# Causal attention and a routed mixture of experts: another order of query halves in the first and the last element, and a lead of the maxima that rises and falls

## The chip, the cores and the metric

The kernel runs on one core of a Trainium2 chip. The metric is the device time of one execution in microseconds (us). A kernel's time is the median of several executions; a profile comes from one execution.

## The reference

The input is x, 4 elements of 1,024 tokens with 256 channels. Attention has 16 heads of 16 channels; its weights are low-rank pairs (down to 64, up to 16), and half of each head's channels of q and k are rotated by position. Then each token goes to two of eight experts. In short:

```
q, k, v = heads of x through down and up, rotary on half of q's and k's channels
scores  = q k^T / sqrt(16), masked to k <= q
y       = softmax(scores) v, joined over the heads
x       = layernorm(x + y Wc)

scores  = (x router_w^T + router_b) / max(temperature, 0.1)       # 8 experts
gates   = exp(sinkhorn(scores, 3 rounds over tokens' and experts' axes, per element))
top two gates of each token, normed to a sum of 1
out     = sum over the two: gate * (relu(x wg_e) * (x wp_e)) wo_e   # 256 -> 512 -> 256
x       = layernorm(x + out)
```

The Sinkhorn rounds and the gates of an element need all of its 1,024 tokens. The experts need all gates of an element.

## The kernel before

**Projection.** Element b is projected in two halves of 512 tokens (project(b, half)). x comes transposed from memory, is split into a high and a low part for matmuls in three terms, and q and k are made and cut into three bf16 pieces each, since later matmuls over the pieces give fp32 precision. The pieces (lv) are written to a scratch in device memory, parts[b], by six DMAs for each half: on SP's queue for element 0, on POOL's for the others. The elementwise steps named lean run on DVE for element 0 and on POOL for the others. v stays on the chip, in va[b % 2].

**Stacks.** Attention is done in units. A unit is an element, one or two groups of four heads, and one or both halves of the queries. load_stack(unit) (L336) reads its pieces back from parts into the tiles qs[i] and ks[i], with i the unit's number modulo 3: 12 DMAs on SP for a one-group unit, 24 for a two-group unit. So the loads of unit i + 3 wait until unit i's matmuls have read the same tiles. load_stack for unit i + 2 is called early in unit i, and at step 30 where unit i + 2 is the first of the next element.

**Maxima.** For each group and half, row_max computes all the scores once, with queries on the partitions (s, L354), and DVE takes the row maxima (L360 off the diagonal, L363 on it). They are transposed, split and written as two more rows of qs by DMAs on ACT's queue. The maxima run ahead of the attention by LEAD steps. A step is one head of one block of 128 keys against 512 queries in the attention, or one head with 128 queries in the maxima.

**Attention.** attend(unit) makes the scores again, with keys on the partitions and minus the maximum included (sT, L433). ACT takes exp into a tile pT (L437), which has three buffers, each with four heads of one key block kb. Diagonal blocks are masked by an affine_select on POOL (L446), or in the last NDV = 2 units by a minimum on DVE (L442). Then come the matmuls y (L417), two blocks behind, and ACT copies the finished y to yT (L422). Keys of block kb with the second half's queries are diagonal for kb 4 to 7.

The units before are: elements 0 to 2, a unit for each group with both halves, 48 steps each; element 3, two units of two groups with the first half of queries (32 steps each), then four units of one group with the second half (32 steps each). In all there are 768 steps.

**Work beside attention.** Two lists of generators are advanced step by step, by budgets. The lane holds the projection of later elements (P), prepare (constants, and the clearing of the pair lists), and finish of the element before (F: transposing y, the output projection, layernorm and the router's scores). The side holds route (R: Sinkhorn, the top two, and the places of the pairs) and lay_out (T: which expert each slot of 256 rows belongs to). The last step of route is 16 scatters of pairs to device memory (L808), on POOL's queue. They are issued only while `hole` is true, in the first eight steps of a second-half part, and in_turn keeps them behind the diagonals that were already emitted on POOL:

```
at = n - HG * BPQ * (len(qcs) - 1)
hole[0] = qcs[-1] > 0 and HOLE[0] <= at < HOLE[1]
```

A scheduler orders the instructions of each engine; every engine then works through its own in order. The maxima have a higher priority.

**The end.** After attention, finish of the last half runs alone, then the last element's route and lay_out, and the slots: 39 slots of 256 rows, of which 35 are always run. Each loads its expert's weights (w), its pairs (ent) and rows (xg), and does gp and eo matmuls. The first 17 slots hold rows of elements 0 to 2 only, and begin right after attention (first gp matmul at 703.7 us in the profile).

Of the kernel before, what the change touches and what calls it, by code (L numbers as in the profile page):

```python
# [17 lines left out]
R_BUFS, X1_BUFS, PT_BUFS, SIDE, SCAT = (1,2,3,0.035,0.07)  # L18
W_BUFS, GA, EA, EO = (2,3,4,6)
SIDE3 = 0.2  # L20
BUD3 = ((8,0,8,0),(4,4,8,8))
YB = 2
XG = 3
SCAT3 = 0.4
# [4 lines left out]
NDV = 2  # L29
HOLE = (0,8)  # L30
PR = (200,0,0)
LEAD = 44
PSUM = bass.MemoryType.PSUM
DRAM = bass.MemoryType.DRAM

P = 128
# [7 lines left out]
def kernel(  # L44
# [189 lines left out]
    def project(b, half, tile_):  # L234
        if half == 0:
            parts[b] = dram.tile([2, NQC, 3, DH, H, QC], BF16, name=f"parts{b}", tag="parts", bufs=2)
        pd = parts[b]
        n = f"{b}_{half}"
        xh = x_half.pop((b, half))
        cols = slice(half * QC, (half + 1) * QC)  # L240
        lean = nc.gpsimd if b else nc.vector
        hi = proj.tile([P, CC, QC], F32R, tag="xT_h", name=f"xT_h{n}")
        lo = proj.tile([P, CC, QC], F32R, tag="xT_l", name=f"xT_l{n}")
        for c in range(CC):
            split(hi[:, c], lo[:, c], xh[:, c], lean)
        yield 0.2
        if half + 1 < NQC or b + 1 < B:
            load_x(b + (half + 1) // NQC, (half + 1) % NQC)

        def chunk(k):  # L250
            ps = tile_(f"qk_ps{n}_{k}")
            cut = slice(k * P, (k + 1) * P)
            mm3(ps, [(wqk_h[:, c, cut], wqk_l[:, c, cut], hi[:, c], lo[:, c]) for c in range(CC)])
            return ps

        def store(k, src, sub, rows):

            lv = proj.tile([P, 3, QC], BF16, tag=f"lv{k}", name=f"lv{n}_{k}")
            nc.scalar.copy(lv[:, 0], src)
            r = proj.tile([P, QC], F32, tag="r", name=f"r{n}_{k}", bufs=R_BUFS)  # L260
            sub.tensor_tensor(r, src, lv[:, 0], ALU.subtract)
            nc.scalar.copy(lv[:, 1], r)
            lean.tensor_tensor(lv[:, 2], r, lv[:, 1], ALU.subtract)
            at = 0
            for qk, row, m in rows:
                (nc.gpsimd if b else nc.sync).dma_start(
                    out=pd[qk, half, :, row : row + m].rearrange("k d h t -> (d h) k t"),
                    in_=lv[at : at + m * H],
                )
                at += m * H  # L270

        for qk in range(2):
            store(2 + qk, chunk(2 + qk), nc.vector, [(qk, 0, DHE)])
            yield 1.3
        pair = []
        for o in range(2):
            pair.append(chunk(o))
            yield 1.3
        for o in range(2):
            t1 = proj.tile([P, QC], F32, tag="t1", name=f"t1_{n}_{o}", bufs=R_BUFS)  # L280
            nc.vector.tensor_tensor(t1, pair[o], rope[:, 2 * o, cols], ALU.mult)
            t2 = proj.tile([P, QC], F32, tag="t2", name=f"t2_{n}_{o}", bufs=R_BUFS)
            nc.vector.tensor_tensor(t2, pair[1 - o], rope[:, 2 * o + 1, cols], ALU.mult)
            lean.tensor_tensor(t1, t1, t2, ALU.add)
            store(o, t1, lean, [(qk, DHE + o * DHE // 2, DHE // 2) for qk in range(2)])
            yield 0.2
        while b >= 2 and not attended.get(b - 2):
            yield WAIT
        dst = va[b % 2][:, half * BPQ : (half + 1) * BPQ, : H * VW]
        for i in range(0, BPQ, 2):  # L290
            ps = tile_(f"v_ps{n}_{i}")
            for j in range(2):
                tok = slice((i + j) * P, (i + j + 1) * P)
                mm3(
                    ps[:, j * C : (j + 1) * C],
                    [(hi[:, c, tok], lo[:, c, tok], wv_h[:, c], wv_l[:, c]) for c in range(CC)],
                )
            for j in range(2):
                nc.scalar.copy(
                    dst[:, i + j].rearrange("p (h d) -> p h d", d=VW)[:, :, :DH],  # L300
                    ps[:, j * C : (j + 1) * C].rearrange("p (h d) -> p h d", d=DH),
                )
            yield 1.3

    units = [(b, (g,), tuple(range(NQC))) for b in range(B - 1) for g in range(NG)]
    units += [(B - 1, (g, g + 1), (0,)) for g in range(0, NG, 2)]
    units += [(B - 1, (g,), (qc,)) for qc in range(1, NQC) for g in range(NG)]

    def stack(unit, g):

# [85 lines left out]
    def attend(unit):  # L398

        b, gs, qcs = unit  # L400
        for g in gs:
            if qcs == (0,):
                y = late_pool[0].tile([P, QC], F32, name=f"yT{b}_{g}_0")
            else:
                y = work.tile([P, T], F32, tag=f"yT{g}", name=f"yT{b}_{g}", bufs=2 if g == 0 else 1)
            for qc in qcs:
                yT[b, g, qc] = y[:, qc * QC : (qc + 1) * QC]
        acc = {}
        behind = []

# [652 lines left out]
                    break  # L1063

    drain(project(0, 0, any_tile))
    load_stack(units[0], (0,))
    drain(project(0, 1, any_tile))
    load_stack(units[0], (1,))
    load_stack(units[1])
    maxima = (1 if step is None else step for u in units for step in row_max(u))  # L1070
    early = project(1, 0, bg_tile)
    attended_to = maxed = 0
    for n in range(HG * BPQ + 1):
        maxed += next(maxima)
# [1 line left out]
            next(early, None)  # L1076

    lane, side = Lane(), Lane()
    lane.add("P1", early)
    lane.add("P1", project(1, 1, bg_tile))  # L1080
    lane.add("prepare", prepare())
    budget = {0: (8.0, 8.0, 8.0, 11.3), 1: (9.5, 9.5, 6.0, 11.3), 2: (9.5, 9.5, 6.0, 0.0)}
    order = [(0, s) for s in range(NA)] + [(1, s) for s in range(NSLOT - NA)]
    sure, more = order[:SURE], order[SURE:]
    early = None

    routed = [0]
    for i, unit in enumerate(units):
        b, gs, qcs = unit
        g = gs[0]  # L1090
        last = b == B - 1
        if g == 0 and qcs[0] == 0 and b > 0:
            if b == 1:
                lane.until("P2h0")
            elif b == 2:
                lane.until("P3h0")
            lane.add(f"F{b - 1}", finish(b - 1))
            if b + 1 < B:
                lane.add(f"P{b + 1}", project(b + 1, 1, bg_tile))
            if last:  # L1100
                lane.until(f"P{b}")
                pctx.close()
                late_pool[0] = pctx.enter_context(tc.tile_pool(name="late", bufs=1, reuse_waits="tile"))
        if g == 1 and 0 < b < B - 1 or g == 0 and last and qcs[0] == 1:
            lane.until(f"F{b - 1}")
        if g == 0 and last and qcs[0] == 1:
            lane.add("F", finish(b, (0,)))
        if g == 3 and b + 2 < B:
            lane.add(f"P{b + 2}h0", project(b + 2, 0, bg_tile))
        steps = len(gs) * sum(HG * BPQ * (qc + 1) for qc in qcs)  # L1110
        give = BUD3[qcs[0]][g] if last else budget[b][g]
        for n, over in enumerate(attend(unit)):
            attended_to += not over
            if i + 2 < len(units):
                if units[i + 2][0] != units[i + 1][0]:
                    if n == 30:
                        lane.until(f"P{b + 1}")
                        load_stack(units[i + 2])
                elif n == 4:
                    load_stack(units[i + 2])  # L1120

            while maxed < min(attended_to + LEAD, HG * BPQ + 3 * attended_to):
                with tc.high_priority(offset=PR[0]):
                    step = next(maxima, None)
                if step is None:
                    break
                maxed += step
            with tc.high_priority(offset=PR[1]):
                lane.give(give / steps)
            if routed[0] < b and not any(m == f"F{b - 1}" for m, _ in lane.todo):  # L1130
                routed[0] = b
                side.add("R", route(b - 1))
                if last:
                    side.add("T", lay_out(0))
            at = n - HG * BPQ * (len(qcs) - 1)
            hole[0] = qcs[-1] > 0 and HOLE[0] <= at < HOLE[1]
            with tc.high_priority(offset=PR[2]):
                side.give(SIDE3 if last else SIDE)
            if last and routed[0] == b and not side.todo and early is None:
                early = pctx.enter_context(early_pool())  # L1140
                fetch(sure[:NA], 0)
        if gs[-1] == NG - 1:
            attended[b] = True
    hole[0] = True
    side.until("T")
    lane.until("F")
# [5 lines left out]
    actx.close()  # L1152
    experts = ctx.enter_context(ExitStack())
    ffn = experts.enter_context(ffn_pool())
    for gen in (finish(B - 1, (1,), alone=True), route(B - 1), lay_out(1)):
        drain(gen)
    filled = nc.values_load(
        tables["filled"][0:1, 0:1], min_val=0, max_val=NSLOT - NA,
# [156 lines left out]
```

## Time and profile before

| what | us |
|---|---|
| time, median of 3 (1090.1 to 1093.66) | 1090.66 |
| the profiled execution's own time | 1088.8 |
| its span | 1087.1 |
| PE busy | 974.8 |
| DVE busy | 821.6 |
| ACT busy | 707.8 |
| POOL busy | 492.4 |
| first load of a stack on SP | 37.1 |
| first s, first sT | 46.5, 66.1 |
| the last yT copy (end of attention) | 702.6 |

Span is the time between the first and the last instruction of the profile, and the mean granted clock of TensorE in it is 0.968 of full speed. Busy times of different engines overlap. An engine's idle time costs nothing unless what it waits for is on the chain that sets the end. Times of single instructions are those of this execution, counted from the start of the span. PEld is TensorE's loading of the fixed operand, which overlaps its matmuls.

### The profile page before, as it was taken

The page shows a single profiled execution, that of the slowest core. Times are in us where ns is not written, and L with a number is a line of the kernel's source. Part 1 is how long each engine was busy: PE and PEld are TensorE (multiplying, and loading weights), DVE is VectorE, ACT ScalarE, POOL GpSimd, SP SyncE. Part 2 cuts the span into 40 slices and gives each one's busy share as a digit, 9 for nine tenths or more (in the row PEclk, how much of TensorE's full clock was granted, in tenths as well). Part 3 has the DMA queues.
Part 4 walks back from the last instruction along what each step waited for, and adds up shares of the span by engine and source line. Part 5 has one row for each costly group of instructions (what it writes and reads, how often), then busy time and mean ns, then how long its engine had stood idle before and what let it go on. Part 6 is the DMA issues. An engine that isn't in the chain of part 4 may idle for free.

```text
span 1087.1 us, 20881 instructions
## 1 busy us (share of the span) xinstructions
PE 974.8 (90%) x6808; PEld 616.2 (57%) x6808; DVE 821.6 (76%) x2551; ACT 707.8 (65%) x1701; POOL 492.4 (45%) x552
## 2 busy tenths in 40 slices
PE   6689999999989999999899999999999699999940
PEld 4444333355434345533344333499999699999940
DVE  4768778888897888887538997398897588888716
ACT  3446666666776665676566776777776577877723
POOL 7167511121443624440423414645557756666545
PEclk9889999999999999999999999999999899999975
DMA  7663411231331312421123220587873788899638
GB/s 258 178 210 112 118 49 35 79 96 44 106 90 48 109 46 74 142 54 50 50 84 121 47 64 2 179 252 214 227 222 101 230 235 237 230 237 255 148 42 309
DMA packets 92065, 146.33 MB, mean 135 GB/s; under 512 B 19760, under 2 KB 55088, under 8 KB 91568
## 3 DMA queue, kind: packets, MB, share of 16 engines
q1 hardware_dynamic: 69296, 108.50, 31.6%
q0 software_dynamic: 20608, 36.18, 14.3%
q8 instruction: 56, 0.92, 0.3%
q10 hardware_dynamic: 2048, 0.27, 0.2%
q14 instruction: 57, 0.47, 0.1%
HBM read 109.26 MB, written 35.38 MB: 133 GB/s over the span
## 4 chain that ended last, share of the span: by engine, by line
PE 68%; DVE 8%; DMA 7%; ACT 6%; issue 4%; POOL 4%; SPq 2%; ACTq 0%; DVEq 0%; POOLq 0%
PE y L417 13%; PE s L354 10%; PE sT L433 9%; PE gp L195 5%; PE gp L196 5%; PE gp L197 5%; ACT pT L437 4%; POOL pairs L808 3%; PE eo L195 3%; PE eo L196 3%; PE eo L197 3%; PE po L591 2%; DVE mx L360 2%; DMA results<-eo,ent 2%; SPq L336 2%
## 5 line engine op out<-in xcount | busy, mean ns | idle before, releaser
L437 ACT ACTIVATE pT<-sT 128x512 f32<-128x512 f32 (+3 forms) x768 | 346.9, 491 | 178.4 <-PE sT L433 151.0
L363 DVE CUSTOM_DVE_ANT_0 d<-s,mask 128x128 bf16<-128x128 f32 (+3 forms) x512 | 237.0, 482 | 51.4 <-PE s L354 50.2
L433 PE MATMUL sT<-qs,ks 98*128 98x512 bf16 (+3 forms) x768 | 231.7, 328 | 16.4 <-ACT pT L437 11.6
L354 PE MATMUL s<-ks,qs 96*128 96x512 bf16 (+3 forms) x768 | 221.9, 331 | 22.5 <-DVE mx L363 7.8
L446 POOL TENSOR_SCALAR_AFFINE_SELECT pT<-pT 128x512 f32<-128x512 f32 x120 | 76.4, 637 | 273.1 <-ACT pT L437 256.8
L360 DVE TENSOR_REDUCE mx<-s 128x1 f32<-128x512 f32 x256 | 175.1, 684 | 29.4 <-PE s L354 28.3
L417 PE MATMUL y<-pT,va 128*32 128x512 f32 (+3 forms) x1536 | 181.9, 500 | 2.0 <-POOL pT L446 0.9
L1010 POOL DMA_INDIRECT results<-eo,ent x70 | 116.9, 1670 | 107.3 <-ACT hh L188 22.1
L189 DVE TENSOR_TENSOR wl<-w,wh 128x512 fp32r<-128x512 f32 x210 | 134.9, 685 | 37.7 <-ACT wh L188 37.4
L195 PE MATMUL gp<-xh,wh 128*128 128x256 f32 x560 | 159.5, 286 | 1.3 <-ACT xh L188 0.7
L197 PE MATMUL gp<-xh,wl 128*128 128x256 f32 x560 | 158.6, 284 | 0.5 <-DVE wl L189 0.5
L196 PE MATMUL gp<-xl,wh 128*128 128x256 f32 x560 | 158.9, 284 | 0.0
L354 PEld LDWEIGHTS <-qs 96*128 96x128 bf16 x768 | 71.6, 99 | 132.8 <-issue 101.0
L433 PEld LDWEIGHTS <-ks 98*128 98x128 bf16 x768 | 71.8, 98 | 122.9 <-issue 91.2
L188 ACT CAST wh<-w 128x512 fp32r<-128x512 f32 x210 | 117.6, 621 | 12.7 <-DMA w<-in_wg_dram 10.9
L195 PEld LDWEIGHTS gp<-xh,wh 128*128 128x128 f32 x560 | 106.0, 190 | 2.4 <-ACT xh L188 1.2
L197 PEld LDWEIGHTS gp<-xh,wl 128*128 128x128 f32 x560 | 106.3, 190 | 0.8 <-DVE wl L189 0.7
L196 PEld LDWEIGHTS gp<-xl,wh 128*128 128x128 f32 x560 | 106.3, 190 | 0.0
L929 POOL DMA_INDIRECT xg<-x_rows,ent x70 | 79.6, 1137 | 37.1 <-issue 17.4
L195 PE MATMUL eo<-wh,hh 128*128 128x256 f32 x280 | 80.1, 286 | 10.4 <-ACT hh L188 9.0
L808 POOL DMA_INDIRECT pairs<-ent,so_i x64 | 66.5, 1039 | 29.6 <-issue 18.4
L196 PE MATMUL eo<-wl,hh 128*128 128x256 f32 x280 | 79.1, 283 | 0.0
(207 smaller groups left out, 1603.1 us busy)
## 6 DMA issues: line engine op xcount, KB each, us to landing
w<-in_wg_dram SPq DMA_DIRECT2D x35, 512.0 KB, 6.2
w<-in_wp_dram SPq DMA_DIRECT2D x35, 512.0 KB, 5.6
w<-in_wo_dram SPq DMA_DIRECT2D x35, 512.0 KB, 4.7
ks<-parts SPq DMA_DIRECT2D x90, 128.0 KB, 2.8
qs<-parts SPq DMA_DIRECT2D x66, 128.0 KB, 2.9
parts<-lv POOLq DMA_DIRECT2D x12, 384.0 KB, 3.1
parts<-lv POOLq DMA_DIRECT2D x24, 192.0 KB, 3.1
xh<-in_x_t_dram SPq DMA_DIRECT2D x8, 512.0 KB, 5.8
```

The lines of the kernel that those rows point to most:

```text
L188: nc.scalar.copy(hi, src)
L189: (sub or nc.vector).tensor_tensor(lo, src, hi.bitcast(F32), ALU.subtract)
L195: nc.tensor.matmul(ps, lhsT=sh, rhs=mh, start=(i == 0), stop=False)
L196: nc.tensor.matmul(ps, lhsT=sh, rhs=ml, start=False, stop=False)
L197: nc.tensor.matmul(ps, lhsT=sl, rhs=mh, start=False, stop=(i == n - 1))
L354: nc.tensor.matmul(ps[:, :w], lhsT=q(h, half)[:NROW, t * P : (t + 1) * P], rhs=k(h, k0 // QC)[:NROW, :w], start=True, stop=True,)
L360: nc.vector.tensor_reduce(m, ps, AX.X, ALU.max)
L363: nc.vector.tensor_tensor_reduce(out=dump[:, :w], in0=ps[:, :w], in1=mask[:, QC - w :], scale=1.0, scalar=MASKED, op0=ALU.add, op1=ALU.max ...
L417: nc.tensor.matmul(acc[g, qc][SLOT * h : SLOT * (h + 1), lo:], lhsT=va[b % 2][:, kb, at : at + SLOT], rhs=pT[:, h, lo:], start=(kb == 0), ...
L433: nc.tensor.matmul(st[:, lo:], lhsT=k(h, kb // BPQ)[: NROW + 2, kb % BPQ * P : (kb % BPQ + 1) * P], rhs=q(h, qc)[: NROW + 2, lo:], start=T ...
L437: nc.scalar.activation(pT[:, h, lo:], st[:, lo:], AF.Exp, scale=scale)
L1010: ins = nc.gpsimd.indirect_dma_start(out=results[:, :], out_offset=bass.IndirectOffsetOnAxis(ap=ent[:, j, 1:2], axis=0), in_=eo, in_offset ...
```

## The change

Element 0 now has the units that element 3 had: two units of two groups with the first half of queries (firsts), then four of one group with the second half (others). Its attention is begun after only the first half has been projected. The second half's projection becomes the first item of the lane, with its lean steps on POOL, and has to be done at step 26 of unit 0, where the loads of unit 2 are issued. The loads of units 0 and 1 (24 DMAs each) are issued before that.

Element 3 has the same units in the other order: the four with the second half of queries first, the two with the first half last. With that, the half that finish takes inside attention is the second and the half that it takes alone is the first. The last two units, which cut their diagonals on DVE, are now the two firsts.

The lead of the maxima is 22 steps at the start, rises by 0.35 for each step of attention to 44, and falls again near the end, from 44 to 22, where it stays for the last 64 steps. Before, it was 44, with a cap of 16 and three for each step at the start. The budgets of the lane are listed by the number of the unit in its element.

```diff
-BUD3 = ((8,0,8,0),(4,4,8,8))
...
-LEAD = 44
+LEAD, SLIM = 44, 22
...
-        lean = nc.gpsimd if b else nc.vector
+        lean = nc.gpsimd if b or half else nc.vector
...
-    units = [(b, (g,), tuple(range(NQC))) for b in range(B - 1) for g in range(NG)]
-    units += [(B - 1, (g, g + 1), (0,)) for g in range(0, NG, 2)]
-    units += [(B - 1, (g,), (qc,)) for qc in range(1, NQC) for g in range(NG)]
+    firsts = [((g, g + 1), (0,)) for g in range(0, NG, 2)]
+    others = [((g,), (qc,)) for qc in range(1, NQC) for g in range(NG)]
+    units = [(0, *u) for u in firsts + others]
+    units += [(b, (g,), tuple(range(NQC))) for b in range(1, B - 1) for g in range(NG)]
+    units += [(B - 1, *u) for u in others + firsts]
...
         for g in gs:
-            if qcs == (0,):
-                y = late_pool[0].tile([P, QC], F32, name=f"yT{b}_{g}_0")
-            else:
+            if b == B - 1 and qcs[0]:
+                yT[b, g, qcs[0]] = late_pool[0].tile([P, QC], F32, name=f"yT{b}_{g}_1")
+            elif (b, g, 0) not in yT:
                 y = work.tile([P, T], F32, tag=f"yT{g}", name=f"yT{b}_{g}", bufs=2 if g == 0 else 1)
-            for qc in qcs:
-                yT[b, g, qc] = y[:, qc * QC : (qc + 1) * QC]
+                for qc in range(NQC):
+                    if (b, g, qc) not in yT:
+                        yT[b, g, qc] = y[:, qc * QC : (qc + 1) * QC]
...
     drain(project(0, 0, any_tile))
-    load_stack(units[0], (0,))
-    drain(project(0, 1, any_tile))
-    load_stack(units[0], (1,))
+    load_stack(units[0])
     load_stack(units[1])
     maxima = (1 if step is None else step for u in units for step in row_max(u))
-    early = project(1, 0, bg_tile)
+    early = project(0, 1, bg_tile)
...
-    lane.add("P1", early)
+    lane.add("P0", early)
+    lane.add("prepare", prepare())
+    lane.add("P1", project(1, 0, bg_tile))
     lane.add("P1", project(1, 1, bg_tile))
-    lane.add("prepare", prepare())
-    budget = {0: (8.0, 8.0, 8.0, 11.3), 1: (9.5, 9.5, 6.0, 11.3), 2: (9.5, 9.5, 6.0, 0.0)}
+    budget = {
+        0: (7.0, 7.0, 4.5, 4.5, 4.5, 6.5), 1: (9.5, 9.5, 6.0, 11.3), 2: (9.5, 9.5, 6.0, 0.0),
+        3: (8.0, 8.0, 0.0, 0.0, 8.0, 8.0),
+    }
...
+    ahead = sum(len(gs) * sum(HG * BPQ * (qc + 1) for qc in qcs) for _, gs, qcs in units)
     for i, unit in enumerate(units):
...
-        if g == 0 and qcs[0] == 0 and b > 0:
+        nth = i - [u[0] for u in units].index(b)
+        if nth == 0 and b > 0:
+            attended[b - 1] = True
...
-        if g == 1 and 0 < b < B - 1 or g == 0 and last and qcs[0] == 1:
+        if nth == 1 and 0 < b < B - 1 or last and g == 0 and qcs[0] == 0:
             lane.until(f"F{b - 1}")
-        if g == 0 and last and qcs[0] == 1:
-            lane.add("F", finish(b, (0,)))
-        if g == 3 and b + 2 < B:
+        if last and g == 0 and qcs[0] == 0:
+            lane.add("F", finish(b, range(1, NQC)))
+        if g == NG - 1 and b + 2 < B:
             lane.add(f"P{b + 2}h0", project(b + 2, 0, bg_tile))
...
-        give = BUD3[qcs[0]][g] if last else budget[b][g]
+        give = budget[b][nth]
         for n, over in enumerate(attend(unit)):
             attended_to += not over
             if i + 2 < len(units):
-                if units[i + 2][0] != units[i + 1][0]:
-                    if n == 30:
+                if i == 0:
+                    if n == 26:
+                        lane.until("P0")
+                        load_stack(units[i + 2])
+                elif units[i + 2][0] != units[i + 1][0]:
+                    if n == 30 if steps > 32 else n == 24:
                         lane.until(f"P{b + 1}")
                         load_stack(units[i + 2])
...
-            while maxed < min(attended_to + LEAD, HG * BPQ + 3 * attended_to):
+            lead = min(LEAD, SLIM + 0.35 * attended_to, SLIM + 0.65 * max(0, ahead - 64 - attended_to))
+            while maxed < attended_to + lead:
...
-        if gs[-1] == NG - 1:
-            attended[b] = True
+    attended[B - 1] = True
...
-    for gen in (finish(B - 1, (1,), alone=True), route(B - 1), lay_out(1)):
+    for gen in (finish(B - 1, (0,), alone=True), route(B - 1), lay_out(1)):
```

## The prediction

> **What bounds the kernel now.** I read the busy shares and the chain first, then the windows of the two stretches that the change rebuilds, then the single lines in them.
>
> ```profile
> PE 974.8 (90%) x6808; PEld 616.2 (57%) x6808; DVE 821.6 (76%) x2551; ACT 707.8 (65%) x1701; POOL 492.4 (45%) x552
> PE 68%; DVE 8%; DMA 7%; ACT 6%; issue 4%; POOL 4%; SPq 2%; ACTq 0%; DVEq 0%; POOLq 0%
> ```
>
> TensorE is 90% busy and carries 68% of the chain. The change leaves every matmul in place, so time can only come from stretches where PE stands or runs slowly, and be lost where PE is made to stand. The windows show those stretches (length, then PE, PEld, DVE, ACT, POOL busy, PEclk):
>
> ```profile
> 25.00:50.00 25.00, 14.65 (x70) 10.44 (x68) 17.79 (x34) 12.10 (x25) 2.52 (x2) 0.88 0.54 159
> 50.00:75.00 25.00, 20.69 (x84) 12.52 (x83) 16.77 (x54) 9.94 (x21) 16.62 (x17) 0.78 0.67 209
> 150.00:200.00 50.00, 47.09 (x291) 16.11 (x290) 39.40 (x141) 32.22 (x77) 8.24 (x13) 1.00 0.19 58
> 650.00:675.00 25.00, 23.68 (x159) 9.27 (x151) 20.65 (x94) 16.13 (x36) 8.45 (x10) 1.00 0.01 2
> 675.00:700.00 25.00, 23.42 (x149) 8.58 (x146) 5.89 (x12) 18.29 (x45) 17.52 (x20) 1.00 0.31 89
> ```
>
> From 25 to 75 us PE is busy 35 of 50 us, at a clock of 0.88 and 0.78: the start has some 15 us of air. At 150 there is hardly any. From 675 PE looks busy, but the scores wait for ACT's exps (18.29 of 25), and DVE is nearly idle since the maxima are all done.
>
> At the start, the key loads (SP) and the granted clock:
>
> ```profile
> L336 SPq DMA_DIRECT2D qs<-parts x24: 536/589/1470, 37.1 to 77.5; - x24
> L336 SPq DMA_DIRECT2D ks<-parts x24: 517/589/818, 38.4 to 78.2; - x24
> ...
> DMA to landing us min/median/max: 2.1/2.3/3.9
> 62.00:64.00 2.00, 0.11 (x1) 1.00 0.31 59
> 64.00:66.00 2.00, 1.48 (x6) 0.65 0.92 309
> 66.00:68.00 2.00, 2.00 (x6) 0.50 0.75 244
> 68.00:70.00 2.00, 2.00 (x7) 0.50 0.74 242
> 70.00:72.00 2.00, 2.00 (x8) 0.64 0.55 168
> ```
>
> Each load holds SP for 0.59 us (0.63 from start to start in a row) and lands some 2.3 us later; half 1's loads wait for its parts. After PE has stood, it gets half its clock for about 6.5 us.
>
> At the end, the 16 scatters of pairs of element 2:
>
> ```profile
> L808 POOL DMA_INDIRECT pairs<-ent,so_i x16: 954/958/1016, 666.6 to 685.6; - x16
> ...
>   DVE need L843: 10.9, 1
>   issue: 4.6, 15
> ```
>
> They go one after the other, 19.0/15 = 1.27 us apart, 3.6 us after the routing's last matmul (so_ps2, at 663). They harm nothing there: the last two units cut their diagonals on DVE (L442), so POOL has no attention behind the scatters.
>
> **The start.** It removes one wait (half 1's projection ahead of all attention), moves half 1's lean work from DVE to POOL, and adds loads: element 0 is loaded by 24+24+12+12+12+12 = 96 DMAs instead of 60. Half 0's parts are ready about 1 us sooner (DVE no longer interleaves half 1's splits), so loads begin at 36.1 instead of 37.1 and the first maxima come at 45.3 (before: 46.5). Two-group unit 0 needs its second group at 52.8 and unit 1 its groups at 60.4 and 68: 12 loads take 7.6 us, and the 16 maxima of a first-half group 6.6 us of DVE, so this about keeps step, and the first scores for exp (sT) come at about 58 instead of 66.1. But all 48 loads stand on SP ahead of half 1's six writes of parts: 36.1 + 48 x 0.635 = 66.6; six writes of 0.73 bring 70.9 (their data, from POOL, would be ready at some 51); five other issues (wc, x, router) of 0.5, to 73.4. The loads of unit 2, the first that needs half 1, wait for the parts to land (74.0), take 12 x 0.65 to 81.8, and land at 84.6. PE, priced by the spacing of its matmuls, comes to unit 2's first maxima at about 78.5, in order, with the last steps of unit 1 behind it: it stands 6 us. By 84.6 it has done 50.9 us of matmul work; before had done 48.9 us at 85.7. So the gain is 2 us of work and 1.1 of time: **-3 us**. The lead's ramp has no cost beside this: with 22 steps of lead, unit 2's maxima are asked for at the end of unit 0 anyway.
>
> Here the Trainium skill speaks for the change. DMA: Bandwidth & Descriptors, section "Issuing engines are not separate DMA queues", holds the sequencer's time for an issue to be usually small beside the DMA. By that rule the 48 loads would hold up nothing, unit 2's keys would come long before 78.5, and the start would gain 3 + 6 = 9 us. The row shows 0.63 us of SP per load of 2.3 us, 30.5 us in all; I take the row. Ends: -9 and +2 (the second group's loads late as well).
>
> POOL takes up half 1's lean work: ten splits, subtracts and adds of 1.2 us (the later elements' rows on POOL), about 12 us in all. I estimate POOL at some 26 busy of 38 us in that stretch with them, so I cost them at nothing; if POOL filled, the diagonals behind them would be late by up to those 12 us. The transposed maxima and their two ACT-queue DMAs per group and half keep their number.
>
> **Elements 1 and 2** keep their units. Budgets and project's order are as before; I cost them at nothing (PE 47 of 50 covers them; ends -1 and +1).
>
> **Stacks in the last element.** A reload takes 12 issues and a landing, 10.0 us from the last use of the stack to the first matmul with the new keys. By the order of PE's instructions the work between these two is 5.8, 6.9, 7.8 and 6.7 us for four of the last units; before, one unit had 6.6 and the rest 9.6 or more. Its one wait of this sort:
>
> ```profile
>   PE s L354: 0.6, 1
>   DMA ks<-parts: 0.5, 1
> ```
>
> By arithmetic, at the 0.83 of that stretch, each of the four is 10 - 6.8/0.83 = 1.8 us short, 7 in all; by the 0.5 us that the one like it cost, 2. I take **+4 us**, ends 0 and 8.
>
> **Pairs ahead of a diagonal.** With the second queries first, element 2's routing ends inside the last second-half unit (group 3), which still cuts its diagonals on POOL, because only the last two units use DVE and these are now the firsts. The order on POOL is: ten scatters, then the diagonals of kb 4 to 7 of that unit, then six scatters. If the routing's last matmul is at T, scatters begin at T+3.6 (as before) and ten take 12.6, so kb 4's diagonal (0.64) ends at T+16.9. On PE, y of kb 4 stands after 17 scores (6, 5, 4 and 2 of widths 512, 384, 256, 128: 5.5 us by 0.38, 0.33, 0.27, 0.22), 11 maxima (3.2 us) and a y (0.6), 9.3 us by durations, which overlap; their 17 exps take 6 x 0.61 + 5 x 0.50 + 4 x 0.39 + 2 x 0.29 = 8.3. So PE is there at about T+8.4 and stands to T+16.9: **+8.5 us**. Behind that y are the rest of group 3, then all of the remaining scores; kb 7's tile is the one that kb 4 holds, so ACT has no buffer and stands as well. What is late next is everything up to the experts: the 63 exps of the firsts behind it (some 25 us) run at ACT's pace, so the time isn't made up. Ends: 3 (the unit arrives late for other reasons) and 12. A stall of that length brings the half clock: over 6.5 us as in 64 to 71, 3.2 us of PE work; TensorE: Matmul & The Clock Gate, section "What's actually happening" in Part 1, lifts the gate after one busy window of about 3.4 us, which would make it 1.7; the row is longer, and I keep to it. Half lies under ACT's work in that tail: **+1.5 us** (0 to 3).
>
> **The rest of the end.** The other six scatters end by about T+29; 2.9 to land, then entries and weights, which took from 688.6 to 703.7, give T+47; PE comes to the experts at T+50 or later, so this chain hides and the first weights are all there: **-1 us**. Finish's part inside attention and its part alone swap halves: the same instructions, with the x load on SP and two stores of 0.8 on POOL, now behind the scatters, where nobody waits for them.
>
> Sum: -3 + 4 + 8.5 + 1.5 - 1 = +10 against the profiled execution's 1088.8 (span 1087.1): 1098.8. That run stood 1.9 under the median 1090.66, so on the median it is about 1100.
>
> **Rivals.** (a) *The shorter lead fills the tail: faster.* Before, the last 47 us did 32.9 us of matmul work, 0.70; with the lead falling to 22, maxima last nearly to the end and DVE, idle now, works beside ACT. At the 0.83 of the stretch before, that work takes 39.6: -7.3. It decides if PE's stand at the diagonals is at its low end (3 us, no half clock): -3 + 4 + 3 - 7.3 - 1 = -4.3, about 1086. For it: DVE's 5.89 of 25. Against it: ACT's exps, not DVE, pace that tail. (b) *It cancels:* start -9, reloads +4, scatters +5: 1090.7. (c) *All waits at their upper ends:* start 0, reloads 8, scatters 12 and clock 3, less 1: +22, about 1112; for it speaks that a late SP queue and a blocked POOL queue have no slack to hide in. That the change doesn't do what it says is excluded: the instruction orders show it.
>
> **How the numbers follow.** A measurement of this kernel tells 0.3% (3.3 us) from no change. My forecast has 0.55 (1094 to 1106), (c) 0.18, (a) 0.17, (b) 0.10. Slower: 0.55 + 0.18 = 0.73; same 0.10; faster 0.17. The range from 1085 to 1110 takes in (a)'s centre, (b) and half of (c).
>
> **What would show it.** Right: a first sT near 58; SP issuing loads without a break from 36 to 66; PE idle near 79 to 85, released by ks<-parts; POOL's L446 of the last second-half unit behind ten L808; PE or PEld of y waiting some 8 us for L446 there, with PEclk at half after it; several waits of s for ks<-parts of 1 to 2 us after 560. Wrong: the first y of unit 2 before 80, or no y waiting for POOL over 3 us, or PE's share in the last 40 us of attention above that of before with the maxima still going.

## The result and the profile after

The changed kernel takes 1127.76 us (1123.43 to 1133.73, 4 runs) against 1091.24 us of the kernel before in the same session: a ratio of 1.0328, 95% interval 1.0274 to 1.0382. The forecast was 1100, in a range from 1085 to 1110. The direction was right; the loss is three and a half times as large. Sessions were of two kinds, the first with before at 1091 to 1093.5 us and a mean clock of 0.97, the second (the "slow chip" of some expectations below) with 1138 and 0.945, and since one chip number, 6, stands for sessions of both kinds, it is not shown that the chip makes the difference.

The profiled execution has a span of 1122.7 us, 35.6 more than before. The last copy of a finished y (yT) is at 740.3 us instead of 702.6. Of these 37.7 us, 2.9 lie in the first stretch of the projection, which differs between executions of one kernel (see below); the rest arises inside attention. From the first to the last gp matmul the experts take 335.5 us, before 336.6. The busy line of the page and the windows that were shown of before, with the one that follows them:

```profile
PE 989.9 (88%) x6808; PEld 623.6 (56%) x6808; DVE 826.4 (74%) x2549; ACT 708.8 (63%) x1701; POOL 499.4 (44%) x554
```

```profile
25.00:50.00 25.00, 13.45 (x66) 9.66 (x65) 13.57 (x22) 9.38 (x21) 10.10 (x8) 0.93 0.41 121
50.00:75.00 25.00, 22.08 (x98) 10.24 (x98) 19.11 (x90) 8.48 (x20) 6.08 (x6) 0.80 0.40 122
150.00:200.00 50.00, 46.41 (x274) 14.91 (x271) 38.92 (x118) 33.10 (x73) 7.99 (x12) 1.00 0.15 43
650.00:675.00 25.00, 23.41 (x153) 8.79 (x150) 21.95 (x123) 15.97 (x37) 3.98 (x5) 1.00 0.25 76
675.00:700.00 25.00, 16.52 (x101) 6.84 (x101) 8.94 (x41) 9.40 (x25) 16.74 (x18) 0.80 0.02 2
700.00:750.00 50.00, 41.11 (x265) 23.35 (x264) 26.02 (x62) 31.52 (x82) 13.02 (x14) 0.80 0.44 142
```

The start is no denser than before (PE 35.5 of 50 us from 25 to 75, before 35.3). The end is much thinner: from 675 to 700 PE is busy 16.5 us instead of 23.4, at a clock of 0.80. The largest waits of PE from 650 to 745 us, and the ones behind them, name what it waited for (total us, times, longest; the last line is of before, 640 to 703 us):

```profile
POOL pairs L810 <- DVE needi L844: 15.1, 1, 15.1
ACT pT L439 <- PE y L419: 11.3, 2, 10.1
PEld y L419 <- POOL pT L448: 9.9, 5, 7.6
PE y L419 <- POOL pT L448: 6.6, 2, 6.3
DVE x L523 <- POOL rstd L521: 5.9, 1, 5.9
PE x1T_ps L583 <- DVE x L523: 4.2, 1, 4.2
...
DVE x L521 <- POOL rstd L519: 7.5, 1, 7.5
```

There are two stands, both on POOL's queue. In before DVE waited for rstd as well, 7.5 us, but PE had no wait behind it. POOL's timeline (start, duration, instruction):

```profile
672.35 1.08 POOL L810 DMA_INDIRECT pairs<-ent,so_i  x1 [15.07 <-DVE needi L844]
...
683.95 0.96 POOL L810 DMA_INDIRECT pairs<-ent,so_i  x1 [0.30 <-issue]
684.92 1.81 POOL L448 TENSOR_SCALAR_AFFINE_SELECT pT<-pT 128x512 f32<-128x512 f32 x3
...
703.27 1.01 POOL L931 DMA_INDIRECT xg<-x_rows,ent  x1 [4.18 <-DMA ent<-pairs]
...
709.92 0.94 POOL L931 DMA_INDIRECT xg<-x_rows,ent  x1 [0.30 <-issue]
710.89 0.27 POOL L520 TENSOR_SCALAR rstd<-mv 128x4 f32<-128x4 f32 x1
711.24 1.05 POOL L521 TENSOR_TENSOR rstd<-rstd,neg_half 128x4 f32<-128x4 f32 x1
```

Ten scatters run from 672.35 to 684.92, and the diagonals behind them run after that, three in a row. In the same way the two small instructions of finish's layernorm (rstd) stand behind six gathers of rows, which waited for their lists. What it does to PE and its clock, in slices of 6 us:

```profile
674.00:680.00 6.00, 4.19 (x17) 1.50 (x16) 4.92 (x35) 3.20 (x8) 4.64 (x5) 0.90 0.03 3
680.00:686.00 6.00, 0.38 (x4) 0.20 (x8) 0.00 (x0) 0.00 (x0) 4.91 (x6) 0.50 0.03 2
686.00:692.00 6.00, 5.30 (x38) 1.32 (x30) 0.00 (x0) 2.45 (x8) 2.33 (x4) 0.74 0.00 0
704.00:710.00 6.00, 3.53 (x19) 1.09 (x17) 1.71 (x5) 3.80 (x9) 4.48 (x6) 0.96 0.86 257
710.00:716.00 6.00, 3.17 (x16) 2.07 (x20) 2.67 (x6) 1.75 (x6) 3.86 (x5) 0.50 1.05 366
716.00:722.00 6.00, 6.00 (x34) 3.41 (x27) 1.51 (x5) 2.44 (x7) 0.00 (x0) 0.50 0.57 211
722.00:728.00 6.00, 6.00 (x35) 3.14 (x34) 3.42 (x11) 4.31 (x10) 2.06 (x2) 0.62 0.15 44
...
688.00:690.00 2.00, 1.69 (x19) 0.56 (x12) 0.00 (x0) 0.48 (x3) 0.00 (x0) 0.73 0.00 0
724.00:726.00 2.00, 2.00 (x14) 0.82 (x13) 1.03 (x3) 1.93 (x4) 1.25 (x2) 0.50 0.00 0
726.00:728.00 2.00, 2.00 (x14) 0.57 (x12) 1.95 (x6) 1.04 (x3) 0.82 (x1) 0.85 0.46 131
```

From 680 to 686 hardly anything but POOL works. Around each stand PE has half its clock. By the shares of the 2 us slices, the half clock ends at 689.1 after the first stand, 3.5 us after PE went on. After the second one it lasts from 709.5 to 726.6, some 17 us, although PE is busy without a gap from 714.

At the start, SP's queue (the last of 48 loads, then half 1's writes) and the two waits of ACT that belong to it (waits of 26 to 110 us):

```profile
70.90 0.59 SPq L337 DMA_DIRECT2D ks<-parts  x1
71.60 4.63 SPq L265 DMA_DIRECT2D parts<-lv  x6
...
ACT lv L258 <- DMA parts<-lv: 2.2, 2, 1.8
```

The loads run without a break from 39.97 to 71.5, and the six writes from 71.6 to 76.2. The wait of ACT looks small, 2.2 us. What stands behind it is element 1's projection: its next pieces go into the same lv tiles, so ACT can make them only when the writes have left, at 74.8. The wait is short because in ACT's order these copies stand behind 11 exps of unit 0 (from 63.8 us on). The matmuls of its first two chunks were done by 57.3, and there is none between that and 76.2.

### The profile page after: what moved, and what is told of

It reads as the page before. It is cut to its first block, busy times and chain, and to the rows that moved or that the text cites. A ratio compares the mean times of both kernels' runs of the same rounds, so it can differ in the third digit from the quotient of the medians.

```text
span 1122.7 us, 20903 instructions
## 1 busy us (share of the span) xinstructions
PE 989.9 (88%) x6808; PEld 623.6 (56%) x6808; DVE 826.4 (74%) x2549; ACT 708.8 (63%) x1701; POOL 499.4 (44%) x554
## 5 line engine op out<-in xcount | busy, mean ns | idle before, releaser
L435 PE MATMUL sT<-qs,ks 98*128 98x512 bf16 (+3 forms) x768 | 234.6, 333 | 19.8 <-ACT pT L439 12.6
L448 POOL TENSOR_SCALAR_AFFINE_SELECT pT<-pT 128x512 f32<-128x512 f32 x112 | 70.9, 635 | 288.5 <-ACT pT L439 279.6
L419 PEld LDWEIGHTS y<-pT,va 128*32 128x32 f32 x1536 | 33.6, 110 | 86.5 <-issue 45.9
```

Of the source, the lines that this page charges most:

```text
L419: nc.tensor.matmul(acc[g, qc][SLOT * h : SLOT * (h + 1), lo:], lhsT=va[b % 2][:, kb, at : at + SLOT], rhs=pT[:, h, lo:], start=(kb == 0), ...
L435: nc.tensor.matmul(st[:, lo:], lhsT=k(h, kb // BPQ)[: NROW + 2, kb % BPQ * P : (kb % BPQ + 1) * P], rhs=q(h, qc)[: NROW + 2, lo:], start=T ...
```

## The experiments

All ratios are to before in the same session, with 95% intervals. A difference of two ratios is uncertain by 0.004 to 0.008, that is 4 to 8 us.

| kernel | first kind | second kind |
|---|---|---|
| changed | 1.0328 (1.0274 to 1.0382) | not run |
| after_again, after_third (the same) | 1.0325 (1.0286 to 1.0365), 1.0314 (1.0256 to 1.0373) | |
| start_only | | 1.0054 (1.0031 to 1.0076) |
| end_only | | 1.0132 (1.0069 to 1.0196) |
| parts_pool | 1.0195 (1.0143 to 1.0247) | |
| start_parts | 1.0049 (1.0026 to 1.0071) | 0.9902 (0.9871 to 0.9934) |
| diag_dve | 1.0202 (1.0155 to 1.0248) | 1.0102 (1.0066 to 1.0138), 1.0056 (1.0033 to 1.0079) |
| gather_after | | 1.0075 (1.0028 to 1.0123), 1.0088 (1.0061 to 1.0115) |
| both_clear | 1.0197 (1.0164 to 1.0229) | |
| end_clear | 1.0123 (1.0095 to 1.0151) | |
| end_lead44 | | 1.0096 (1.0058 to 1.0134), 1.0047 (1.0021 to 1.0074) |
| all_clear | 1.0066 (1.0045 to 1.0087) | 1.0003 (0.9985 to 1.0021) |

Single executions of one kernel differ by several us in two places that have nothing to do with the change: the first stretch, up to PE's pause of 1.0 us ahead of the first projection matmul of half 1 (it begins at 25.4, 28.2 and 27.6 us in three executions of the changed kernel, 25.3 in before), and the stretch after the last eo matmul (41.2, 35.0 us; before 42.3). Where traces are compared below, the first gp matmul is counted from that first point, set to before's: it is at 703.7 in before, and 35 to 38 us later in the changed kernel.

**The two halves of the change.** start_only has element 3 and the end of the lead as before, end_only has element 0 as before (the leading line of each edit; budgets, finish's halves and the load order go with it):

```diff
# start_only
-    units += [(B - 1, *u) for u in others + firsts]
+    units += [(B - 1, *u) for u in firsts + others]
...
# end_only
-    units = [(0, *u) for u in firsts + others]
+    units = [(0, (g,), tuple(range(NQC))) for g in range(NG)]
```

> Only element 0 is changed (its halves of queries, the load order, the lean work on POOL, the lead from 22); element 3 and the end of the lead are as before. Theory: the ends of elements 0, 1 and 2 came 4.7, 9.1 and 10.3 us later in the changed kernel, all of it from this part, so about 1101. Rival (my prediction's sum): this part gains 3, and the delay up to element 2 comes from elsewhere: about 1088.

> Only element 3 is changed (second queries first, the lead falling at the end); element 0 is as before. Theory: the end carries its loss whatever the start does: attention of element 3 took 27.4 us longer in the changed kernel and what follows 2.1 less, so about 1116. Rival: the stands at the end come from the late start (queues shifted against each other), and this kernel stays under 1105.

Each half loses time by itself (1.0054 and 1.0132). Both ran in the second kind only, where the changed kernel was not run, so they give the sign and not the sizes. The rival for the start, a gain of 3 us, is excluded there.

**One stand each.** diag_dve cuts the diagonals of the last second-half unit on DVE; gather_after moves the gathers behind rstd:

```diff
# diag_dve
-NDV = 2
+NDV = 3
...
# gather_after
-    def in_turn(ins):
+    def in_turn(ins, diagonal=diagonal):
...
-        nc.gpsimd.tensor_tensor(rstd, rstd, neg_half, ALU.pow)
+        normed[0] = nc.gpsimd.tensor_tensor(rstd, rstd, neg_half, ALU.pow)
...
-                in_turn(ins)
+                in_turn(ins, normed)
...
-            if last and routed[0] == b and not side.todo and early is None:
+            if last and routed[0] == b and not side.todo and early is None and not any(m == "F" for m, _ in lane.todo):
```

> The changed kernel with the diagonals of the last second-half unit on DVE too (3 units instead of 2), so that no diagonal stands behind the scatters of pairs on POOL. Theory: the stand of PE at 678 to 686 us (7.4 us) goes, with the half clock after it (5 us at half): about 10 less than the changed kernel, 1117. Rival: PE then stands at the next thing on POOL (layernorm's rstd behind the gathers) or waits for ACT, and no more than 3 us are gained.

> The changed kernel with the gathers of rows (xg) placed on POOL behind layernorm's rstd of finish, instead of before it. Theory: PE's stand of 4.2 us at 709 to 713 and the half clock from 709 to 723 go: 4 plus up to 7, about 1119. Rival: that tail is paced by ACT's exps, and only the 4 us or less go: 1124 or more.

These two came out in the second kind (1.0102, 1.0075) and told nothing about their share, for want of the changed kernel there.

**Both stands, the end without the start, and SP's order.** both_clear has both edits above. end_clear is both_clear with element 0 as before. parts_pool changes one line of the changed kernel:

```diff
-                (nc.gpsimd if b else nc.sync).dma_start(
+                (nc.gpsimd if b or half else nc.sync).dma_start(
```

> The changed kernel itself once more, beside the three that undo parts of it, on one chip. The first comparison gave 1.033 of before (1127.8 to 1091.2). The four runs so far were on a chip where before took 1138 instead of 1091, and gave 1.005 (start alone), 1.013 (end alone), 1.010 and 1.008 (one stand removed each). Theory: the loss belongs to the kernel and adds up from the parts, so on the slow chip this gives about 1.019, on one like the first 1.033. Rival: the loss was a matter of that chip, and this is within 1.01.

> The changed kernel with both stands at the end removed: the last second-half unit's diagonals on DVE, and the gathers of rows behind layernorm's rstd on POOL. Theory: 7.4 + 4.2 us of standing and 5 + 14 us at half clock, of which half counts: about 19 less than the changed kernel, that is a ratio 0.017 lower than after_again's. Rival: one of the two hides behind the other or behind ACT's exps, and at most 8 us (0.007) are gained.

> Element 0 as before; only the end is changed, and both of its stands are removed as in both_clear. Theory: what is left of the end's loss is the stack reloads (2.8 + 2.1 us seen) and the slower mixture of 640 to 690, less 2 at the experts: 3 to 6 over before, ratio 1.003 to 1.006. Rival (the order of element 3 pays once POOL's queue is clear): below 0.997.

> The changed kernel with the six writes of half 1's parts in element 0 issued on POOL's queue instead of SP's, so that they don't stand behind the 48 key loads. In the changed kernel they were issued at 71.6 to 76.2 us, and ACT's first copy of element 1's projection waited for them at 74.8 (ACT lv <- DMA parts<-lv). Theory: element 1's projection can start at about 57 and fill PE while DVE makes the maxima: the end of unit 0 comes some 5 us earlier, ratio 0.005 below after_again's. Rival: DVE's maxima fill 50 to 74 anyway and nothing moves: within 0.002.

The loss belongs to the kernel: 1.0325 again. Both stands are worth 0.013, that is 14 us, give or take 6: between the 19 that I took and the rival's 8, neither of which this excludes. The surprise is parts_pool: one queue for another in six DMAs is worth another 0.013, 14 us, give or take 7, where I expected 5. Its trace shows a part of the reason. The projection's matmuls of 48 to 90 us, in the changed kernel (first two lines: count, then start of the first and last) and in parts_pool (last two):

```profile
L194 PE MATMUL qk_ps<-xT_h,wqk_h x8: 388/448/792, 52.3 to 82.8; 128*128 128x512 f32 x8
L195 PE MATMUL qk_ps<-xT_l,wqk_h x8: 389/490/647, 53.8 to 83.3; 128*128 128x512 f32 x8
...
L194 PE MATMUL qk_ps<-xT_h,wqk_h x14: 387/398/504, 52.9 to 88.3; 128*128 128x512 f32 x14
L195 PE MATMUL qk_ps<-xT_l,wqk_h x14: 389/397/587, 55.1 to 88.6; 128*128 128x512 f32 x14
```

In the same time 14 of each instead of 8. ACT copies element 1's pieces at 57.8 and 58.3 instead of 74.8 and 76.1 (first line the changed kernel, second parts_pool):

```profile
74.80 0.59 ACT L258 CAST lv<-qk_ps 128x512 bf16<-128x512 f32 x1 [1.75 <-DMA parts<-lv]
...
57.82 1.07 ACT L258 CAST lv<-qk_ps 128x512 bf16<-128x512 f32 x2 [3.34 <-PE qk_ps L196]
```

So the time while DVE makes the maxima (DVE is busy 5.4 and 5.3 of 6 us from 57 to 63) is filled with work that the changed kernel has to do later, when PE is nearly full (46.4 of 50 us from 150 to 200). From the traces: the first gp comes 23 us after before's in both_clear and 9 in end_clear, which differ by the start alone: 14.5 (by the times 0.0074, 8 us). In parts_pool it comes 22 after, 13 to 16 less than in the changed kernel. So undoing SP's order brings back about as much as the start loses.

But only half of that lies at the start. The copies of a finished y tell where an element ends (each has eight; count, first and last start; the first three lines are after_again, the last three parts_pool):

```profile
L424 ACT COPY yT<-y x8: 580/591/602, 81.3 to 235.1; 128x512 f32<-128x512 f32 x8
L424 ACT COPY yT<-y x24: 558/592/616, 81.3 to 568.9; 128x512 f32<-128x512 f32 x24
L424 ACT COPY yT<-y x32: 558/592/629, 81.3 to 740.7; 128x512 f32<-128x512 f32 x32
...
L424 ACT COPY yT<-y x8: 560/586/592, 87.7 to 231.7; 128x512 f32<-128x512 f32 x8
L424 ACT COPY yT<-y x24: 560/586/631, 87.7 to 565.1; 128x512 f32<-128x512 f32 x24
L424 ACT COPY yT<-y x32: 560/586/631, 87.7 to 727.3; 128x512 f32<-128x512 f32 x32
```

Counted in this way, from that first point to the end of element 0, from there to the end of element 2, and on to the first gp (one trace each, three of the changed kernel; all_clear in the first kind of session, told below):

| us | before | changed | parts_pool | both_clear | end_clear | all_clear |
|---|---|---|---|---|---|---|
| element 0 | 209.3 | 209.8 to 211.1 | 203.6 | 213.2 | 207.2 | 207.4 |
| elements 1 and 2 | 327.8 | 332.3 to 333.8 | 333.4 | 333.8 | 333.5 | 335.4 |
| element 3 | 141.3 | 168.8 to 172.9 | 163.4 | 154.8 | 146.5 | 146.1 |

SP's line brings 6 to 7.5 us in element 0 and 5.4 to 9.5 in element 3 (parts_pool against the changed kernel), or 6 and 9 (all_clear against both_clear). The reading above explains the first part. In element 3 the two kernels differ in nothing that was edited, but the scheduler lays all of attention anew: about two thirds of PE's matmuls there can be matched in order, while two traces of the changed kernel match in full. PE's waits for reloads in element 3 are then 2.0 us instead of 4.7 to 4.9, and half clock lasts 24 us instead of 31 to 41. Whether this part belongs to the late writes or to the order that happened to come out is not shown. Elements 1 and 2 take 4.5 to 7.6 us longer than in the one trace of before, whatever was undone; why is open.

end_clear is 13 us over before (9 by the trace: 5.7 in elements 1 and 2, 5.2 in element 3, less 2.1 in element 0); the theory of 3 to 6 was too low, and the rival (the order pays once POOL is clear) is excluded. A new stand appears in it. The waits of PE, 570 to 735 us:

```profile
PE sT L435 <- DMA qs<-nm: 3.6, 1, 3.6
PE sT L435 <- ACT pT L439: 3.0, 11, 0.5
PE s L355 <- DMA ks<-parts: 2.0, 2, 1.1
```

The first is the transposed maximum of the last group, written by ACT's queue while expert weights are loaded (DMA share 1.03 from 690 to 700); the wait is from 701 to 704, and from 705 to 710 the clock is 0.55. In after_again the same wait was 0.7 us, in both_clear it is 3.1: it comes up where the two stands are removed.

**The sum, the lead, the start with its cause undone.** all_clear is both_clear with parts_pool's line. end_lead44 is end_clear without the falling lead. start_parts is start_only with parts_pool's line.

```diff
# end_lead44
-            lead = min(LEAD, HG * BPQ + 2 * attended_to, SLIM + 0.65 * max(0, ahead - 64 - attended_to))
+            lead = min(LEAD, HG * BPQ + 2 * attended_to)
```

> The changed kernel with all three undone: parts of element 0's half 1 written through POOL's queue, the last second-half unit's diagonals on DVE, the gathers behind layernorm's rstd. Counted from the same point of the start, the first expert matmul came 35 to 38 us later than before in the changed kernel, 23.4 in both_clear, 22 in parts_pool, 8.8 in end_clear. Theory: the parts add up (14.5 for SP's order, 13.5 for the two stands, 9 for the rest of the end), so about 9 over before: 1.008. Rival: the early start only brings the end's stands forward and part of the 14.5 is lost again: over 1.015.

> end_clear with the lead of the maxima kept at 44 to the end instead of falling to 22. In end_clear PE stood 3.6 us at 701 to 704 for a transposed maximum (PE sT <- DMA qs<-nm) and had half its clock after it. Theory: with 44 steps of lead that wait goes: 5 us less, ratio 1.0075 against 1.0123. Rival (what the shorter lead was to bring: more maxima beside the exps of the tail): the kernel is slower than end_clear, 1.015 or more.

> Only element 0 is changed, with half 1's parts written through POOL's queue; element 3 as before. In parts_pool the ends of elements 0, 1 and 2 came 5.7 and 3.1 us before and level with those of before, counted from the same point of the start. Theory: the front half's gain is used up by the work that it puts off: 0.998 to 1.003. Rival: 5 us are kept, 0.995 or less, and this kernel is the fastest of all.

> diag_dve again, on the same chip as others: the changed kernel with only the stand behind the scatters removed. both_clear removed two stands and came out 13.8 us better. Theory: this one is 7.4 us of standing and some 3 of clock, 10 of the 13.8: ratio 1.023. Rival: the second stand (rstd behind the gathers) simply takes over, and it is within 4 us of the changed kernel: 1.029 or more.

All four fell in the second kind of session, and were inconclusive for what they were meant to settle: all_clear 1.0003, start_parts 0.9902. There, the engines stand for a good part of the time that scatters take. start_parts from 691 to 715 us, while 16 scatters run on POOL from 691.6 to 711.9, then the 20 us of these scatters as a whole, and (last line) the same 16 scatters of the same kernel in the first kind of session (start_parts_b, 672.1 to 692.8):

```profile
691.00:697.00 6.00, 6.00 (x37) 2.85 (x31) 4.62 (x31) 3.20 (x7) 4.20 (x5) 1.00 0.03 4
697.00:703.00 6.00, 0.80 (x3) 0.21 (x2) 1.26 (x4) 1.13 (x3) 4.66 (x5) 0.91 0.03 2
703.00:709.00 6.00, 2.76 (x13) 0.54 (x12) 1.16 (x2) 1.28 (x4) 4.60 (x5) 0.50 0.03 2
709.00:715.00 6.00, 0.15 (x1) 0.00 (x0) 0.00 (x0) 0.47 (x3) 3.56 (x5) 0.50 0.03 2
691.60:711.90 20.30, 8.97 (x47) 3.60 (x44) 6.44 (x32) 5.40 (x13) 15.70 (x17) 0.75 0.03 2
...
672.10:692.80 20.70, 19.06 (x107) 6.00 (x103) 7.45 (x33) 15.88 (x36) 16.10 (x16) 1.00 0.03 3
```

From 697 to 715 PE is busy 3.7, DVE 2.4 and ACT 2.9 of 18 us, with no diagonal on POOL behind the scatters. It is not as bad in every trace of that kind: end_lead44's PE is busy 17.5 of the 21.7 us of its 16 scatters. A wait for POOL during scatters may therefore cost less there, since part of that time is lost anyway; this was not measured.

The same kernels beside the changed one, in the first kind:

> The changed kernel beside three that undo parts of it. On chips where before takes 1138, all engines stand while scatters of pairs go (18 us around 706 in start_parts)[...]. Theory: the loss is the kernel's own: 1.033 where before takes 1091; where before takes 1138, 1.018 to 1.026, since the three kernels with one part undone had 1.006 to 1.010 there. Rival: there the changed kernel is within 1.012, and the order at the end costs nothing where the scatters stop everything anyway.

> Element 0 changed, half 1's parts written through POOL's queue, element 3 as before; 0.990 of before where before takes 1138. Theory: that gain belongs to those chips; where before takes 1091 the front half's gain is used up by element 2: 0.997 to 1.003. Rival: 0.994 or less on either.

> The changed kernel with all three causes undone; 1.000 of before where before takes 1138. Theory: where before takes 1091 the parts add up as counted from the traces (14.5 for SP's order and 13.5 for the two stands off 36): 1.008. Rival: they overlap, 1.015 or more.

> The changed kernel with only the stand behind the scatters removed; 1.006 to 1.010 of before where before takes 1138. Theory (my prediction's largest term, 8.5 and 1.5 for the clock): 10 us, so 0.009 below after_third on the same chip. Rival: the second stand takes over, and it is within 0.004 of after_third.

The parts add up within their uncertainty: with all three undone the ratio is 1.0066, and 0.0314 less 0.013 (SP's order) less 0.013 (stands) is 0.0054. diag_dve alone takes 0.011, 12 us, give or take 8, nearly all of what the two stands are worth. It still has a stand of 5.4 us in front of x1T, at 702 to 708. By the traces its first gp is 2 us later than both_clear's; by the times the two kernels can't be told apart. start_parts is 5 us slower than before, so no version that was tried beats before in the first kind; in the second, start_parts is 1% faster than before.

**What was still open.**

> The changed kernel with only the gathers of rows moved behind layernorm's rstd on POOL; where before takes 1091 it is not measured yet (1.008 where before takes 1138). The stand behind the scatters alone was worth 0.011 (1.0202 against 1.0314), both together 0.013. Theory: the two overlap: with the first stand still there, this one is worth 4 us of standing and some of the half clock after it, 1.024 to 1.028. Rival: it is worth only the 0.002 that is left between the two: 1.029 or more.

> end_clear with the lead kept at 44 to the end; 1.0096 where before takes 1138. end_clear had 1.0123 where before takes 1091, with a stand of 3.6 us for a transposed maximum at 701. Theory: that wait goes with the longer lead: 1.005 to 1.009. Rival: the shorter lead pays elsewhere and this is 1.012 or more.

Both fell in the second kind again (1.0088 and 1.0047). So what the second stand is worth alone, and what the falling lead costs, is not settled there. In neither trace of end_lead44 does PE wait for a transposed maximum over 0.9 us, which fits the theory; the price does not follow from that.

## Why the prediction was wrong, and where it was right

Its sum was -3 + 4 + 8.5 + 1.5 - 1 = +10. Measured, in the first kind of session: +36.

- **The start, -3: wrong in sign; it is +14 by the traces (8 by the times).** The failing step is the end of that paragraph: "PE comes to unit 2's first maxima at about 78.5 ... it stands 6 us. By 84.6 it has done 50.9 us of matmul work". Priced in the same way, an estimate of the work done by the first yT copy at 85.8 is 42.1 us, where before had done 48.9 at 85.7 (2.9 us of this trace's delay lie in the first stretch). SP's order itself was read well: the writes were forecast from 66.6 to 70.9 and unit 2's loads from 74.0 (measured 71.6 to 76.2, and 79.3). But I asked only who waits for unit 2's keys. The writes were late for another reader of the same buffers: ACT, which needs the lv tiles back for element 1's projection. No wait for unit 2's keys over 0.9 us is in the trace, since PE came there later. Of the 14, some 7 are lost in element 0 in this way, and the other part is lost in element 3, under another instruction order, for a reason that stays open. With the writes on POOL's queue element 0 is 5.7 us shorter than before, more than the gain forecast. A second slip is small: the loads began at 39.97, not 36.1, but 2.9 us of that are the first stretch (36.95 in after_again). Before had half 1's projection in the gaps of half 0's; PE now waits in them (3.5, 1.4 and 2.8 us from 33 to 46).
- **Elements 1 and 2, nothing (-1 to +1): wrong by 4.5 to 6**, and by 5.6 to 7.6 in the kernels with parts undone. The term was left at nothing because units and budgets stay as they were; the cause is open, and there is one trace of before to compare with.
- **The rule of the Trainium skill** (DMA: Bandwidth & Descriptors, "Issuing engines are not separate DMA queues"). By the rule that issuing is usually small beside the DMA the start was to gain 9; the row of 0.63 us per load was right against it (48 loads, 31.5 us), and even it was used too narrowly.
- **Pairs ahead of a diagonal, 8.5 and 1.5 for the clock: right.** The routing's last matmul is at 669.8. Scatters were forecast 3.6 us later, PE at the y at 8.4 and going on at 16.9; they came at 2.5, PE is through with what stands before that y at 679.3 (9.5), and goes on at 685.6 (15.8). Undone, 12 us come back, give or take 8, against 10 forecast. The clock was nearer to the shorter of the two figures that the prediction weighed: 3.5 us at half after PE went on, 1.7 us of work; part of the half clock fell into the stand.
- **"Nobody waits for them": wrong.** I placed finish's x load and stores behind the scatters and left out finish's two rstd instructions, which stood behind six gathers of rows that I had not placed either, and which DVE, PE and so the whole of attention wait for: 4.2 us and 17 us of half clock. Its price with the first stand in place is open; without it, about 2.
- **Stack reloads, +4: right in size**, in two waits instead of four: 2.8 us for ks<-parts at 579 and 2.1 at 610 (labelled qs<-nm, where that unit's loads were still running). In parts_pool and end_clear only 2.0 are left, so the size hangs on the rest of the order; that it met +4 is partly luck.
- **The experts, -1: right**, 1.1, 0.4 and 0.3 less from the first to the last gp in the three traces.
- **The rest of the end**, some 3 us of element 3 in end_clear beyond its reloads: not in the sum. A part of it is the wait for a transposed maximum with 22 steps of lead; the share is open.
- **The rivals.** (a), the shorter lead filling the tail, has no support: in the last 47 us of attention PE is busy 41.1 us in end_clear and 43.9 in before, and a maximum comes late in it. (c), all waits at their upper ends, was nearest with 1112, and its reason, that late queues have no slack, is what happened; the start lay outside its bounds.

The range failed mainly because the start's ends, -9 and +2, were set around one consumer of the late writes; the second stand and elements 1 and 2 had no price. The change as a whole would have been within 1% of before if six DMAs and one unit's diagonals had been on other queues and six gathers behind two small instructions.

## What to carry to other kernels

When a DMA is moved behind others in a queue, list everything that waits for it to finish, the reuse of its source buffer first: here the writer's tiles were needed back before anyone needed the data. On a queue in order, small compute instructions that sit between long runs of indirect DMAs inherit all of their time, so trace each one to its reader when a phase is moved. A short wait in the list (2.2 us on ACT) may be what is left of a longer delay of other work: here some 7 us in that element. And where a scheduler lays the order, one changed line moves instructions far away: compare runs stretch by stretch before giving a whole difference to the line.

## What the runs showed of the hardware

- Half clock may last far longer than the stand that it comes with: 17 us, from 709.5 to 726.6, where PE stood 4.2 us and was busy without a gap from 714. After the stand of 6.3 us it ended 3.5 us after PE went on. Why the two differ is not shown.
- Sessions differ by more than the change. Before takes 1091 to 1093.5 us in one kind and 1138 in the other. While 16 scatters of pairs run, PE of one and the same kernel is busy 9.0 of 20.3 us in the slower kind (start_parts) and 19.1 of 20.7 in the faster, with "issue" or "remote" named as the releaser of many of the waits. Why is not shown, and no trace of before was taken in the slower kind. A ratio measured in one kind can't be set beside one from the other: start_parts is 0.990 in one and 1.005 in the other.
